# Slots of a counted graph layer put in order of segment size, and their byte parts cut out by one shift with three amounts

## The chip, the cores and the metric

One core of a Trainium2 chip runs the whole program. The metric is the device time of one execution in microseconds (us), median of three runs. For the kernel before these are 1352.64, 1352.75 and 1355.45 us. The profile is of a further execution, which took 1350.42 us; its recorded span is 1348.7 us, so 1.7 us lie outside the records.

## The reference

12,500 nodes have rows of 128 features. Each of 200,000 edges, sorted by destination, sends the normalized row of its source through one of four matrices to its destination:

```python
h = jnp.maximum(_layernorm(x, axis=-1), 0.0)
for i in range(4):
    mask = (edge_types == i)[:, None]
    msgs = msgs + jnp.where(mask, h[src] @ W[i] + b[i], 0.0)
x = x + jax.ops.segment_sum(msgs, dst, num_segments=N)
```

Destinations are drawn as `12500 * u**2`, so low node numbers have many edges and high ones few.

## The kernel before, in words

The edges are cut into 1563 chunks of 128. The last 995 chunks are *gathered*: GpSimd (POOL) fetches 128 rows of the normalized table `htab` per chunk by an indirect DMA (L614, 947 chunks; the first 48 take rows of x instead, L598), and TensorE (PE) sums them by one-hot matmuls (L667). Ten buffers of two chunks each hold the rows, so a gather waits until PE has used up the pair ten places earlier. The first 568 chunks are *counted*: for each of 1705 low nodes the kernel counts how often each source row and type occurs (one-hots on VectorE, L1092 and L1102; a matmul, L1127; a copy of the counts by ScalarE, L1135) and multiplies the counts by the table (from L1233 on).

What is counted together is a *slot*: one chunk seen from one unit of nodes. A unit is one node, or two or three neighbouring nodes whose counts share one 32-bit word, a byte each. Six segments of nodes follow each other in node order, with these sizes of a unit: nodes 0 to 3 size 1 (up to 16 chunks each), 3 to 117 size 3 (up to 12), 117 to 393 size 1, 393 to 462 size 3 (two chunks), 462 to 1036 size 2, 1036 to 1705 size 3. There are 850 units and 1035 slots. Slots are numbered in blocks (L145 to L152): first chunk k = 0 of all segments, then k = 1 of those that have it, and so on to k = 15. From k = 2 on a block of size 1 (nodes 0 to 3) and a block of size 3 (nodes 3 to 117) take turns, down to blocks of one slot.

`make_slots` fills the slots before the counting can begin. Three of its steps matter here:

- `runs(a, z)` (L957 to L966) cuts a stretch of slots into runs of one size, joining neighbours of equal size.
- `pick_out` (L968) works on three stretches of slots, 0 to 425 and 425 to 850 twice each and 850 to 1035 once. After its matmuls (L975, L978) it evicts each run apart: a square on ScalarE (ACT) into `off`, since the middle of the unit depends on the size (L986), then a compare-and-multiply on VectorE (DVE) into `packed` or `mask` (L987).
- `unpack` (L999) works on four pieces, slots 0 to 41, 41 to 317, 317 to 676 and 676 to 1035. It makes columns of constants for the counting (L1002 to L1022), then a matmul sums the edges of each type into a 12-row result (L1028). For each run, ScalarE casts the sums to integers (`ints`, L1036), VectorE takes the bytes out by a mask, a shift in place, a mask, a shift, a mask (L1041 and L1040, five instructions for size 3 and three for size 2), and ScalarE copies them to `cnt12` and adds them up on the way (L1043, two records each: the copy and the read of its accumulator). A run of size 1 goes straight from the sums to `cnt12`.

At the end a matmul with the bias per piece of a segment (L1059) and a copy (L1063) fill the first sums `acc`. All of this is written ahead of the main part. In the main part PE, VectorE and ScalarE work in the order of the program text; ahead of it a list scheduler that builds the program lays out each engine's queue, and may set instructions of the main part between those of the slots. The table (L532, L558, L568, L574) and three groups of raw rows (L725 and around it) are made in the same stretch of time. `gates` hold nineteen pairs of gathers back until marked instructions of `pick_out` and `unpack` are done.

Of the kernel before, what the change touches and what calls it, by code (L numbers as in the profile page):

```python
# [35 lines left out]
F32 = mybir.dt.float32  # L36
# [5 lines left out]
I32 = mybir.dt.int32  # L42
U16 = mybir.dt.uint16
AF = mybir.ActivationFunctionType
ALU = mybir.AluOpType
# [5 lines left out]
P = 128  # L51
# [37 lines left out]
def kernel(  # L89
# [10 lines left out]
    nc = tc.nc  # L100
    N, D = x.shape
    E = src.shape[0]
    NT, _, DO = w.shape
# [7 lines left out]
    N3 = 3 * NT  # L111
# [11 lines left out]
    ND = int(N * q**2 + 5 * 2 * q * N * (q * (1 - q) / E) ** 0.5) // 8 * 8 + 8  # L123

    def chunks_of(d, n):

        m = E * (((d + n) / N) ** 0.5 - (d / N) ** 0.5)
        return max(1, -(-int(m + ODDS * m**0.5) // P))

    ONES = next(d for d in range(0, ND, 3) if chunks_of(d, 1) == 1)  # L130
    TWOS = next(d for d in range(ONES, ND, 3) if chunks_of(d, 2) == 1)
    THREES = next(d for d in range(TWOS, ND, 2) if chunks_of(d, 3) == 1)
    NTWO = (THREES - TWOS) // 2
    HEAVY = next(d for d in range(0, ND, 3) if E * (((d + 1) / N) ** 0.5 - (d / N) ** 0.5) < 4 * P)
    parted = [(d, k) for d in range(HEAVY) for k in range(0, chunks_of(d, 1), 3)]
    LONE = next(n for n in range(min(NTWO - len(parted), TWOS - ONES), -1, -1) if (TWOS - ONES - n) % 3 == 0)
    AFTER = ONES + LONE
    ND += -(ND - THREES) % 3
    assert 0 < HEAVY < ONES <= AFTER <= TWOS < THREES < ND < 2047
    segs = []  # L140
    for d0, d1, size in ((0, HEAVY, 1), (HEAVY, ONES, 3), (ONES, AFTER, 1), (AFTER, TWOS, 3), (TWOS, THREES, 2), (THREES, ND, 3)):
        segs.append((sum(n for _, n, *_ in segs), (d1 - d0) // size, d0, size, [chunks_of(d, size) for d in range(d0, d1, size)]))
    UNITS = sum(n for _, n, *_ in segs)
    blocks = {}
    NS = 0  # L145
    for k in range(max(segs[0][4])):
        for s in range(len(segs)):
            n = sum(c > k for c in segs[s][4])
            if n:
                assert all(c > k for c in segs[s][4][:n])  # L150
                blocks[k, s] = NS, n
                NS += n  # L152
    assert (1, 2) not in blocks and segs[2][2:4] == (ONES, 1)
    LONE0 = blocks[0, 2][0]
    LONE1 = LONE0 + LONE

    def weight_at(c):
        return c if c < LONE0 else c - LONE

    ends_in = [12, 8, 4, 3]  # L160
    FULL = (TM - sum(ends_in)) // G
# [11 lines left out]
    size_of = lambda d: next(size for _, n, d0, size, _ in segs if d0 <= d < d0 + n * size)  # L173

    def slot_at(k, d):
        s = next(s for s in reversed(range(len(segs))) if d >= segs[s][2])
        return blocks[k, s][0] + (d - segs[s][2]) // segs[s][3]

    def slots_of(u):

        got = []
        u = list(zip(u, (1.0, 256.0, 65536.0)))
        if u[0][0] is not None and size_of(u[0][0][0]) > 1:
            d = u[0][0][0]
            size = size_of(d)
            got += [(slot_at(k, d), None) for k in range(chunks_of(d, size))]
            del u[:size]
        for v, by in u:
            if v is not None:
                d, k0 = v  # L190
                got += [(slot_at(k, d), by) for k in range(k0, min(k0 + 3, chunks_of(d, 1)))]
        return got
# [115 lines left out]
    prep = early.enter_context(tc.tile_pool(name="prep", bufs=1))  # L308
# [159 lines left out]
    nc.vector.tensor_copy(minus_h, minus)  # L468
    minus_1 = prep.tile([1, P], F16, name="minus_1")
    nc.vector.memset(minus_1, -1.0)  # L470
    mids = prep.tile([P, 3], F32, name="mids")
    for n in range(3):
        nc.vector.memset(mids[:, n : n + 1], -n / 2)
# [426 lines left out]
    def make_slots(dix):  # L900

        def pieces(a, z, of=512):
            n = -(-(z - a) // of)
            return [(a + (z - a) * i // n, a + (z - a) * (i + 1) // n) for i in range(n)]

        d1 = dix.tile([P, NS], F16, name="d1")
# [38 lines left out]
        for u0, n, _, _, caps in segs:  # L945
            i = 0
            while i < n:
                m = sum(c == caps[i] for c in caps)
# [8 lines left out]
        def runs(a, z):  # L957
            got = []
            for (_, s), (c0, n) in blocks.items():
                r0, r1, size = max(a, c0), min(z, c0 + n), segs[s][3]  # L960
                if r0 < r1:
                    if got and got[-1][2] == size:
                        r0 = got.pop()[0]
                    got.append((r0, r1, size))
            return got
# [33 lines left out]
        def unpack(a, z, shared):  # L999
            n = z - a  # L1000
            xi = dix.tile([P, 512], I32, name="xi")[:, :n]
            nc.vector.tensor_single_scalar(xi, packed[:, a:z], 256.0, op=ALU.mult)  # L1002
            hk = dix.tile([P, 512], I32, name="hk")[:, :n]
            nc.vector.tensor_single_scalar(hk, xi, 10, op=ALU.arith_shift_right)
            marks.append(nc.vector.tensor_copy(hkT[:, a:z], hk).ins)
            lo = dix.tile([P, 512], I32, name="lo")[:, :n]
            nc.vector.tensor_single_scalar(lo, xi, 255, op=ALU.bitwise_and)
            marks.append(nc.vector.tensor_single_scalar(loT[:, a:z], lo, -1.0, op=ALU.add).ins)
            if shared:
                by = byT[:, weight_at(a) : weight_at(a) + n]  # L1010
                nc.vector.tensor_single_scalar(xi, xi, 768, op=ALU.bitwise_and)
                nc.vector.tensor_single_scalar(xi, xi, float(1 << 18), op=ALU.mult)
                nc.vector.tensor_single_scalar(by.bitcast(I32), xi, float(127 << 23), op=ALU.add)
            nc.vector.tensor_single_scalar(hk, hk, NT - 1, op=ALU.bitwise_and)
            ohs = []
            for t in range(NT):
                is_t = dix.tile([P, 512], BF16, name="sel", bufs=2 * DENSE)[:, :n]
                of, like, op = (hk, t + 1.0, ALU.is_equal) if t < NT - 1 else (hkT[:, a:z], 0.5, ALU.is_gt)
                if shared:
                    one = nc.vector.scalar_tensor_tensor(is_t, of, like, by, op0=op, op1=ALU.mult)  # L1020
                else:
                    one = nc.vector.tensor_single_scalar(is_t, of, like, op=op)  # L1022
                ohs.append(is_t)
            marks.append(one.ins)
            yield True
            pn = x_ps.tile([N3, 512], F32, name="pt")
            for t in range(NT):
                nc.tensor.matmul(pn[:, :n], pick_a[:, t, :], ohs[t], start=(t == 0), stop=(t == NT - 1))  # L1028
            for r0, r1, size in runs(a, z):
                k, s, c0 = next((k, s, c0) for (k, s), (c0, m) in blocks.items() if c0 <= r0 < c0 + m)  # L1030
                w0 = at_nodes[k, s] + (r0 - c0) * size
                to = cnt12[:, w0 : w0 + (r1 - r0) * size]
                of = pn[:, r0 - a : r1 - a]
                if size > 1:
                    ints = dix.tile([N3, 512], I32, name="ints")[:, : r1 - r0]
                    nc.scalar.copy(ints, of)  # L1036
                    of = dix.tile([N3, 3 * 512], I32, name="parts", bufs=2)[:, : (r1 - r0) * size]
                    for m in range(size):
                        if m:
                            nc.vector.tensor_single_scalar(ints, ints, 8, op=ALU.arith_shift_right)  # L1040
                        nc.vector.tensor_single_scalar(of[:, m::size], ints, 255, op=ALU.bitwise_and)  # L1041
                i = len(some_of)
                some_of.append(nc.scalar.activation(to, of, AF.Copy, accum_out=some[:, i : i + 1]))  # L1043

        for r0, r1 in ((0, LONE0), (LONE0, LONE1), (LONE1, NS)):
            for a, z in pieces(r0, r1):
                yield from unpack(a, z, r0 != LONE0)
                yield True
# [4 lines left out]
        for s, (_, n, d0, size, _) in enumerate(segs):  # L1053
            for a, z in pieces(0, n * size):
                pn = x_ps.tile([P, 512], F32, name="pt")
                todo = [(at_nodes[k, r], m * size) for (k, r), (_, m) in blocks.items() if r == s and m * size > a]
                for i, (w0, m) in enumerate(todo):
                    m = min(m, z)
# [333 lines left out]
    slots = mid.enter_context(tc.tile_pool(name="slots", bufs=1, side="right"))  # L1392
    loT = slots.tile([P, NS], F32, name="loT")
    hkT = slots.tile([P, NS], F32, name="hkT")
    byT = slots.tile([P, NS - LONE], F32, name="byT")
    building = ExitStack()
    dix = building.enter_context(tc.tile_pool(name="dix", bufs=1, side="right"))
    to_slots = make_slots(dix)
    work = None
    dense_out = False  # L1400
# [299 lines left out]
    with tc.If(rv > 0):  # L1700
        with tc.tile_pool(name="slow", bufs=1) as slow, tc.tile_pool(name="slow_ps", bufs=1, space=PSUM) as slow_ps:
# [31 lines left out]
            with tc.For_i(0, T, 1) as t:  # L1733
                d1 = slow.tile([P, 1], F32, name="d1")
# [88 lines left out]
```

## Time and profile before

| what | value |
|---|---|
| median of 3 runs | 1352.75 us |
| profiled execution, whole | 1350.42 us |
| profiled execution, span | 1348.7 us |
| PE, share of the span busy | 90% |
| VectorE (DVE) | 80% |
| ScalarE (ACT) | 79% |
| POOL | 71% |
| DMA | 322.56 MB at a mean of 239 GB/s |

A share over the whole span says little here, because the program has stages. From the start to about 87 us the table is made; then slots and the first rows are made and counted; from about 165 us on counting, table products and gathers run beside each other until the end. Groups of instructions are listed by line with their count, busy time, mean duration and the idle time of the engine just ahead of them; a window view gives the busy time of each engine in a stretch; a timeline gives each instruction's start, its duration and, in brackets, how long its engine had been idle and who ended that. A start stands first in a row of the timeline, then the duration, both in us; runs of equal instructions are merged with a count.

### The profile page before, as it was taken

The numbers are of one execution on the slowest core, as the hardware profiler recorded it, in microseconds if no ns is written. First come the engines' busy times: TensorE is split into PE (matmuls) and PEld (weight loads), VectorE is DVE, ScalarE is ACT, GpSimd is POOL, SyncE is SP. The second block draws the span as 40 slices with busy tenths as digits, with TensorE's granted clock in tenths as the row PEclk, the third lists the DMA queues.
The fourth block names the chain that finished last, engine by engine and source line by source line (L and its number), as shares of the span: only waits on it lengthen the run. The fifth ranks groups of instructions, "written<-read, shape, count | busy, mean of one in ns | idle before, by whom it ended". The sixth has DMA issues, their size and how long they took to land. (4 is left out here: it accounts for less than half of the span.)

```text
span 1348.7 us, 30484 instructions
## 1 busy us (share of the span) xinstructions
PE 1219.8 (90%) x9211; PEld 879.8 (65%) x9211; DVE 1078.0 (80%) x5297; ACT 1068.3 (79%) x1893; POOL 956.0 (71%) x1035
## 2 busy tenths in 40 slices
PE   4875875799999999999999999999999999999975
PEld 1433654477777777777777777776676777667753
DVE  8996476977898898898988888788878888776532
ACT  6894743598998998989889888888978888778731
POOL 7735454677777777777777777777777777777774
PEclk9995677799999999999999999999999999999996
DMA  8743299598888888888788887878878887778952
GB/s 249 231 152 110 59 313 324 164 286 256 278 266 264 278 251 258 257 270 278 240 260 257 261 248 251 259 242 254 252 228 253 254 254 233 241 222 266 325 145 79
DMA packets 184630, 322.56 MB, mean 239 GB/s; under 512 B 30243, under 2 KB 82524, under 8 KB 184460
## 3 DMA queue, kind: packets, MB, share of 16 engines
q1 hardware_dynamic: 132716, 214.63, 48.9%
q0 software_dynamic: 46992, 96.30, 25.0%
q10 hardware_dynamic: 4752, 9.64, 1.8%
q8 instruction: 73, 1.20, 0.4%
q14 instruction: 97, 0.79, 0.2%
HBM read 294.78 MB, written 25.67 MB: 238 GB/s over the span
## 5 line engine op out<-in xcount | busy, mean ns | idle before, releaser
L614 POOL DMA_INDIRECT hm<-htab,srcT x947 | 902.3, 953 | 356.0 <-issue 189.8
L1195 ACT ACTIVATE dec<-counts 128x1116 fp32r<-128x1116 uint8 (+1 forms) x594 | 676.2, 1161 | 5.0 <-PE pa L1233 4.6
L1092 DVE TENSOR_SCALAR o<-iota_w,hkT 128x392 bf16<-128x392 f16 x1035 | 422.6, 408 | 115.7 <-PE pt L1127 112.7
L1233 PE MATMUL pa<-dec,hs 128*128 128x372 f32 x1764 | 389.1, 354 | 0.0
L1241 PE MATMUL pa<-counts,hs 128*128 128x372 fp8e4 x1764 | 341.6, 327 | 5.6 <-ACT sd L1279 5.6
L1135 ACT CAST counts<-pt 128x396 int32<-128x396 f32 x571 | 285.2, 519 | 42.1 <-PE pt L1127 22.5
L1233 PEld LDWEIGHTS pa<-dec,hs 128*128 128x128 f32 x1764 | 301.8, 188 | 13.8
L1127 PE MATMUL pt<-o,o 128*128 128x396 bf16 x1035 | 277.1, 340 | 16.9 <-DVE o L1102 11.4
L1241 PEld LDWEIGHTS <-hs 128*128 128x128 f16 x1764 | 164.5, 96 | 118.3 <-issue 9.1
L1102 DVE TENSOR_SCALAR o<-iota_b,loT,byT 128x128 bf16<-128x128 bf16 x730 | 239.3, 328 | 0.0
L756 DVE TENSOR_TENSOR ring<-ring,py 128x18 f32 (+6 forms) x912 | 158.6, 174 | 60.6 <-issue 16.1
L667 PEld LDWEIGHTS <-hm 128*128 128x128 f16 x2841 | 146.1, 100 | 87.3 <-DMA hm<-htab,srcT 23.6
L667 PE MATMUL ps<-oh,hm 128*128 128x72 bf16 (+7 forms) x2841 | 182.7, 200 | 17.8 <-DMA hm<-htab,srcT 17.3
L657 ACT ACTIVATE sb<-ps 128x288 f32<-128x288 f32 (+8 forms) x237 | 103.3, 436 | 111.4 <-PE py L693 90.3
L632 DVE TENSOR_SCALAR oh<-iota_b,keyT 128x72 bf16<-128x72 bf16 (+7 forms) x947 | 161.6, 259 | 8.6 <-PE ps L667 8.5
L693 PE MATMUL py<-sb,wsb 128*128 128x288 f32 (+6 forms) x456 | 123.9, 416 | 0.0
L1127 PEld LDWEIGHTS <-o 128*128 128x128 bf16 x1035 | 81.9, 99 | 55.0 <-DVE o L1102 17.8
L693 PEld LDWEIGHTS py<-sb,wsb 128*128 128x128 f32 x456 | 85.4, 198 | 22.5 <-issue 0.9
L1102 DVE TENSOR_SCALAR o<-iota_b,loT 128x128 bf16<-128x128 bf16 x305 | 83.3, 273 | 0.0
L598 POOL DMA_INDIRECT hx<-in_x_dram,srcT x48 | 46.4, 967 | 20.2 <-issue 10.8
L688 ACT CAST cnt<-pt 128x288 bf16<-128x288 f32 (+10 forms) x62 | 25.9, 418 | 42.0 <-PE pt L684 37.2
L1263 PE MATMUL pa<-counts,hs 128*128 128x156 fp8e4 x294 | 31.2, 261 | 18.7 <-DMA hs<-htab 18.5
(252 smaller groups left out, 819.3 us busy)
## 6 DMA issues: line engine op xcount, KB each, us to landing
hs<-dtab SPq DMA_DIRECT2D x576, 288.0 KB
hm<-htab,srcT POOLq DMA_INDIRECT x947
htab<-h SPq DMA_DIRECT2D x32, 288.0 KB
hs<-htab SPq DMA_DIRECT2D x32, 288.0 KB
dtab<-dec ACTq DMA_DIRECT2D x32, 288.0 KB
xo<-in_x_dram SPq DMA_DIRECT2D x23, 256.0 KB
out_dram<-xo SPq DMA_DIRECT2D x23, 256.0 KB
hm<-in_x_dram SPq DMA_DIRECT2D x18, 192.0 KB
```

The costliest lines, as they stand in the source:

```text
L614: one = nc.gpsimd.indirect_dma_start(out=hm[:, (i - h0) * D3 : (i - h0 + 1) * D3], out_offset=None, in_=htab, in_offset=bass.IndirectOffse ...
L632: nc.vector.tensor_scalar(oh[:, i, :], iota_b[:, :K], keyf[:, at : at + 1], None, ALU.is_equal)
L667: nc.tensor.matmul(ps[:, i - i0, :], rows(i, c), oh[:, i, :], start=(c == 0), stop=(c == 2))
L693: nc.tensor.matmul(py[:, :g, :], wsb[:, t, :], sb[0][:, :g, t, :], start=False, stop=(t == NT - 1))
L756: nc.vector.tensor_tensor(to, to, of(i), ALU.add)
L1092: one = nc.vector.tensor_scalar(o2[:, k, :NB].rearrange("p (r n) -> p r n", r=ROWS), iota_w, hkT[:, s : s + 1], None, ALU.is_equal)
L1102: one = nc.vector.tensor_scalar(o1[:, k], iota_b, loT[:, s : s + 1], by, ALU.is_equal, ALU.mult)
L1127: one = nc.tensor.matmul(pb, o1, o2, start=first, stop=last)
L1135: lambda i=i, pb=pb: nc.scalar.copy(counts[:, :, i * NT : (i + 1) * NT], pb.rearrange("p (b t) -> p b t", t=NT))
L1195: nc.scalar.activation(decoded[n][:, : j1 - j0, :nv].rearrange("p j (m v) -> p j m v", m=3), by_digit[:, j0:j1, : nu * NT * 4].rearrange(" ...
L1233: nc.tensor.matmul(to.rearrange("p (m v) -> p m v", m=3), row.bitcast(F32R)[:, D // 2 :], decoded[j // DS][:, j % DS, :nv].rearrange("p (m ...
L1241: nc.tensor.matmul(to.rearrange("p (m v) -> p m v", m=3), row[:, :D], counts[:, j, : nu * NT * 4].rearrange("p (v m) -> p m v", m=4)[:, :3 ...
```

## The change

The six segments stand in another order, with all of one size together: size 2 (nodes 462 to 1036) first, then the three of size 3 (3 to 117, 393 to 462, 1036 to 1705), then the two of size 1 (117 to 393, 0 to 3). The blocks of later chunks follow the same idea: behind the 850 units come the later chunks of nodes 0 to 3 (26 slots, size 1, so that they continue the stretch of size 1 ahead of them), then all later chunks of size 3 (159 slots). `unpack` takes four pieces again: slots 287 to 571 (size 3), 0 to 287 (size 2), 571 to 876 (size 1, without the weight `byT`, which is 29 columns shorter now) and 876 to 1035 (size 3). The rule of `runs` is the same; the stretches that it finds are others. Worked out from the text: `pick_out` meets 10 runs in its five jobs in place of 37, `unpack` 4 runs in place of 30 (three with bytes in place of 16).

The second edit is in `unpack`: a small table `shifts` (0, 8, 16 in each of 12 rows) is made once by POOL, and in place of three or five instructions one shift with two tensors writes all bytes, and one mask follows.

```diff
-    for d0, d1, size in ((0, HEAVY, 1), (HEAVY, ONES, 3), (ONES, AFTER, 1), (AFTER, TWOS, 3), (TWOS, THREES, 2), (THREES, ND, 3)):
+    for d0, d1, size in ((TWOS, THREES, 2), (HEAVY, ONES, 3), (AFTER, TWOS, 3), (THREES, ND, 3), (ONES, AFTER, 1), (0, HEAVY, 1)):
...
-    for k in range(max(segs[0][4])):
-        for s in range(len(segs)):
-            n = sum(c > k for c in segs[s][4])
...
+    for k, s in (
+        *((0, s) for s in range(len(segs))),
+        *((k, len(segs) - 1) for k in range(1, max(segs[-1][4]))),
+        *((k, s) for k in range(1, max(map(max, (of[4] for of in segs)))) for s in range(len(segs) - 1)),
+    ):
+        n = sum(c > k for c in segs[s][4])
...
-    LONE0 = blocks[0, 2][0]
-    LONE1 = LONE0 + LONE
+    PAIRS = segs[0][1]
+    LONE0 = segs[4][0]
+    LONE1 = UNITS + sum(segs[5][4]) - HEAVY
+    LONES = LONE1 - LONE0
...
+    shifts = prep.tile([N3, 3], I32, name="shifts")
+    nc.gpsimd.iota(shifts, pattern=[[8, 3]], base=0, channel_multiplier=0)
...
-                    for m in range(size):
-                        if m:
-                            nc.vector.tensor_single_scalar(ints, ints, 8, op=ALU.arith_shift_right)
-                        nc.vector.tensor_single_scalar(of[:, m::size], ints, 255, op=ALU.bitwise_and)
+                    nc.vector.tensor_tensor(
+                        of.rearrange("p (i m) -> p i m", m=size),
+                        ints.unsqueeze(2).to_broadcast([N3, r1 - r0, size]),
+                        shifts[:, :size].unsqueeze(1).to_broadcast([N3, r1 - r0, size]),
+                        ALU.arith_shift_right,
+                    )
+                    nc.vector.tensor_single_scalar(of, of, 255, op=ALU.bitwise_and)
...
-        for r0, r1 in ((0, LONE0), (LONE0, LONE1), (LONE1, NS)):
+        for r0, r1 in ((PAIRS, LONE0), (0, PAIRS), (LONE0, LONE1), (LONE1, NS)):
```

More of the change, by code (lines that the diff above doesn't have):

```diff
@@ L145 @@
     NS = 0
-    for k in range(max(segs[0][4])):
-        for s in range(len(segs)):
-            n = sum(c > k for c in segs[s][4])
[L149 to L153, printed above, removed]
-    LONE0 = blocks[0, 2][0]
-    LONE1 = LONE0 + LONE
+    for k, s in (
[4 more added lines that the diff above has]
+        n = sum(c > k for c in segs[s][4])
+        if n:
+            assert all(c > k for c in segs[s][4][:n])
+            blocks[k, s] = NS, n
+            NS += n
+    PAIRS = segs[0][1]
+    LONE0 = segs[4][0]
+    LONE1 = UNITS + sum(segs[5][4]) - HEAVY
+    LONES = LONE1 - LONE0
+    assert max(segs[4][4]) == max(segs[0][4]) == max(segs[3][4]) == 1
     def weight_at(c):
-        return c if c < LONE0 else c - LONE
+        return c if c < LONE0 else c - LONES
     ends_in = [12, 8, 4, 3]
@@ L175, in slot_at @@
     def slot_at(k, d):
-        s = next(s for s in reversed(range(len(segs))) if d >= segs[s][2])
+        s = next(s for s, (_, n, d0, size, _) in enumerate(segs) if d0 <= d < d0 + n * size)
         return blocks[k, s][0] + (d - segs[s][2]) // segs[s][3]
@@ L1394 @@
     hkT = slots.tile([P, NS], F32, name="hkT")
-    byT = slots.tile([P, NS - LONE], F32, name="byT")
+    byT = slots.tile([P, NS - LONES], F32, name="byT")
     building = ExitStack()
```

## The prediction

> **What bounds the kernel now.** I read the page first, then busy time by stage, then POOL's timeline, then the timelines of ACT and DVE in the stretch that stood out. The columns of the stage view are the stretch, its length, the busy time (and count) of PE, of PE's weight loads, of DVE, ACT and POOL, the granted PE clock, the DMA share and GB/s.
>
> ```profile
> span 1348.7 us, 30484 instructions
> ```
>
> ```profile
> 60.00:87.00 27.00, 20.90 (x81) 9.01 (x79) 26.07 (x119) 26.97 (x73) 7.85 (x9) 1.00 0.61 210
> 87.00:102.00 15.00, 11.33 (x77) 7.35 (x76) 14.68 (x80) 13.53 (x55) 8.22 (x9) 0.86 0.31 99
> 102.00:113.00 11.00, 9.83 (x42) 6.33 (x42) 8.48 (x37) 3.53 (x15) 9.17 (x7) 0.50 0.74 244
> 113.00:133.00 20.00, 6.58 (x39) 3.34 (x38) 13.49 (x73) 8.92 (x68) 7.13 (x8) 0.50 0.17 44
> 133.00:165.00 32.00, 25.55 (x156) 20.84 (x156) 10.76 (x48) 23.20 (x66) 13.86 (x15) 0.59 0.22 57
> 258.00:1326.00 1068.00, 1036.67 (x8063) 761.94 (x8061) 870.90 (x4282) 908.12 (x1413) 808.09 (x853) 0.99 0.81 252
> ```
>
> Each stage has its own limit. From 60 to 87 ACT is full (26.97 of 27 us, the table) and DVE nearly so. From 258 to 1326 us PE is busy 97% and POOL issues 853 gathers in 1068 us, 1.25 us each. From 113 to 133 us nothing is full: PE works 6.58 of 20 us, DMA stands at 17%, and DVE and ACT hand work to each other. POOL's timeline says what that stretch costs.
>
> ```profile
> 121.32 0.95 POOL L614 DMA_INDIRECT hm<-htab,srcT  x1 [0.30 <-issue]
> 133.02 0.94 POOL L614 DMA_INDIRECT hm<-htab,srcT  x1 [10.76 <-PE ps L667]
> ...
> 161.87 0.94 POOL L614 DMA_INDIRECT hm<-htab,srcT  x1 [2.64 <-PE ps L667]
> ...
> 258.05 0.94 POOL L614 DMA_INDIRECT hm<-htab,srcT  x1 [3.28 <-PE ps L667]
> ```
>
> The view of waits gives POOL's for 122 to 163 us in one row (total, times, longest):
>
> ```profile
> POOL hm L614 <- PE ps L667: 26.1, 6, 10.8
> ```
>
> A gather of 0.95 us and 0.30 us of issue make the 1.25 us: behind 258.05 POOL never waits longer than that issue, so the end is set by when this last unbroken run starts. Until then its long waits are for PE's use of earlier rows (L667), never for its own work. So a microsecond by which the main part starts earlier should be a microsecond off the end. The main part starts when the slots are done:
>
> ```profile
> 113.03 0.28 ACT L1036 CAST ints<-pt 12x174 int32<-12x174 f32 x1
> ...
> 115.73 0.64 ACT L1043 ACTIVATE cnt<-parts 12x522 bf16<-12x522 int32 x1 [2.27 <-DVE parts L1041]
> ...
> 128.99 0.13 ACT L1036 CAST ints<-pt 12x1 int32<-12x1 f32 x1
> ...
> 130.03 0.21 ACT L1043 ACTIVATE cnt<-parts 12x3 bf16<-12x3 int32 x1 [0.76 <-DVE parts L1041]
> 130.15 0.18 ACT L1043 ACTIVATION_READ_ACCUMULATOR cnt<-parts 12x1 f32 x1
> 130.24 0.13 ACT L1036 CAST ints<-pt 12x1 int32<-12x1 f32 x1
> ...
> 133.38 0.49 ACT L1135 CAST counts<-pt 128x396 int32<-128x396 f32 x1
> ```
>
> ```profile
> 129.16 0.14 DVE L1041 TENSOR_SCALAR parts<-ints 12x1 int32<-12x1 int32 x1 [0.41 <-ACT ints L1036]
> ...
> 129.86 0.14 DVE L1041 TENSOR_SCALAR parts<-ints 12x1 int32<-12x1 int32 x1
> ```
>
> One run of a single slot takes a round: cast at 128.99, five dependent instructions on DVE from 129.16 to 130.00, the copy at 130.03, the next cast at 130.24. That is 1.25 us for one column. The last piece has 24 such runs, and its chain lasts from 113.03 to the first cast of counts at 133.38, 20.35 us.
>
> **The change part by part.** The groups, from 40 to 135 us (count, busy us, mean ns, idle ahead):
>
> ```profile
> L1041 DVE TENSOR_SCALAR parts<-ints 12x1 int32<-12x1 int32 (+12 forms) x47 | 9.1, 195 | 6.3 <-ACT ints L1036 5.5
> L1040 DVE TENSOR_SCALAR ints<-ints 12x1 int32<-12x1 int32 (+12 forms) x31 | 5.4, 174 | 0.8
> L987 DVE SCALAR_TENSOR_TENSOR packed<-off,pt 128x1 f32<-128x1 f32 (+14 forms) x30 | 4.6, 181 | 1.7 <-ACT off L986 1.6
> L986 ACT ACTIVATE off<-pt,mids 128x3 f32<-128x3 f32 (+14 forms) x37 | 9.2, 291 | 2.1 <-DVE packed L987 1.8
> L1063 ACT COPY acc<-pt 128x287 f32<-128x287 f32 (+6 forms) x8 | 2.7, 337 | 2.5 <-PE pt L1059 2.5
> ```
>
> ```profile
> L708 DVE TENSOR_TENSOR ohf<-iota_f,keyT 128x768 fp32r<-128x768 f32 x1 | 0.9, 944 | 0.0
> L1007 DVE TENSOR_SCALAR lo<-xi 128x359 int32<-128x359 int32 x2 | 0.7, 326 | 0.0
> ```
>
> *New byte step.* 78 instructions (47 and 31, 14.5 us busy) become three shifts and three masks, on 852, 574 and 477 elements of 12 rows. No shift with two tensors is in the trace. Its nearest row is L708, which also reads two stretched operands: 944 ns for 768 elements, in proportion 1.05, 0.71 and 0.59 us. A mask is at most in proportion to L1007: 0.77, 0.52 and 0.43 us. Together 4.1 us. From below, all six could be as cheap as the mean of the old ones, 195 ns, 1.2 us; from above I double to 8.2 us, because integers and 12 rows are not the row's case. I take 4.1 us, nearest to rows of the same access and size. For a large run the edit by itself even loses a little (five instructions of 284 elements, 0.26 us each by L1007, are 1.3 us against 1.8); what gains is that there are three runs and not sixteen.
>
> *The chain at the end.* The last piece has one run now. By rows: cast 0.28, shift 0.59, mask 0.43, copy of 477 elements 0.64 (the row for 522), accumulator 0.18. The copies of `acc` still to come behind it, four of eight because a buffer of PSUM serves each in turn, take (2.7 + 2.5) / 8 = 0.65 us each with their wait, 2.6. With some 0.2 us for hand-overs that is 4.9 us in place of 20.35: **15.4 us** off. With the shift doubled it is 14.4.
>
> *Ahead of 113 us.* 27 of the 37 pairs of square and compare go. DVE loses the idle time of the stage 102 to 113, 11 minus 8.48 = 2.5 us, most of it the 1.6 us behind L986 in the row of L987: **2.5 us**. Of its busy time the 27 take 27 x 0.18 = 4.9 by their means, but the ten that stay are larger and cover the same slots, and small ones overlap; I take **1.2 us** (from 0 to 3). On ACT the first two jobs, which stand among the work on the table, lose six of ten squares: at 0.29 each 1.7; some filled idle moments, so **1.0 us** earlier for the table. The byte step costs as much as before there: 18 old instructions of about 0.19 against the first two new pairs, 3.05; nothing either way. Sum 4.7 us.
>
> *Moved.* The first counted batch takes units of the last segment, whose slots come with the first piece now, so its one-hots can be made sooner. That is worth nothing while DVE is full, and up to 4 us if they leave the last pieces' way. The gates of the gathers keep their number, three marks per piece and four pieces; the wait at 133.02 is for PE, so they are not last. In the main part no instruction changes in number: units and batches are the same, only slot numbers differ.
>
> *At nothing.* One iota on POOL at the start:
>
> ```profile
> 2.00 0.15 POOL L455 IOTA cidx_i<- 128x5 int32 x1
> ...
> 4.31 1.11 POOL L598 DMA_INDIRECT hx<-in_x_dram,srcT  x1 [1.26 <-ACT srcT L349]
> ```
>
> Such a one takes 0.15 us and hides in POOL's wait of 1.26; uncovered it costs 0.15.
>
> *What is late next.* The six waits of 26.1 us hold 6 x 0.3 of issue, so POOL stood 24.3 us for PE. Without any of it the gather of 161.87 could start at 137.6 by POOL's own rate; PE, 20.1 us earlier, releases its buffer for 141.8. So PE still comes last there, by 4.2 us, and POOL's later run starts earlier by the whole shift.
>
> *Sum.* 15.4 + 4.7 = 20.1 us. The profiled execution would go from 1348.7 + 1.7 = 1350.4 to 1330.3; its like among the runs has a median 2.3 us higher, so I put 1352.75 - 20.1 = **1332.6 us**.
>
> *The clock.* Two more rows, same columns:
>
> ```profile
> 104.00:108.00 4.00, 3.90 (x22) 3.06 (x22) 3.09 (x17) 1.38 (x6) 3.39 (x3) 0.50 0.76 243
> 164.00:168.00 4.00, 3.68 (x38) 3.19 (x38) 3.90 (x17) 2.71 (x7) 2.89 (x4) 1.00 0.28 75
> ```
>
> PE gets half its clock at 104 although it is busy 3.90 of 4 us, and the whole of it at 164; I let the slow stretch move along unchanged. [...]
>
> **The rivals.** *POOL takes over.* If the gathers were bound by their own rate from 122 on, only the first wait would be won, 10.76 - 0.3 = 10.5 us: 1342.3. For it: POOL sets the pace later. Against: five more waits for PE follow, to 161.87, with 15.3 of the 26.1 us.
>
> *The clock returns early.* From 133 to 165 PE is busy 25.55 us at 0.59, 15.1 us at full clock; ACT's 23.20 us of work then bound the stage of 32, so up to 8.8 us more: 1323.8.
>
> *Slower.* DVE works its queue in order. A large shift set early in it waits for ACT's cast, and ACT is full from 60 to 87 with the table; behind the shift stands the last split of each table block (L574), so the table would wait too. If DVE stood 25 us there, the result is 1352.75 - 20.1 + 25 = 1357.7; it decides from 20.1 us of standing. Against: work on the slots stood in DVE's queue there before, with squares of ACT to wait for, and DVE was busy 26.07 of 27 us.
>
> *It doesn't do what it says.* If the runs did not merge, or the next stage had its own start, the time stays 1352.75. The count of runs follows from the text, so this is small.
>
> **How the numbers follow.** Forecast 0.75, POOL 0.08, clock 0.10, slower 0.04, nothing 0.03. The forecast's own terms reach from 14.4 + 2.5 = 16.9 to 15.4 + 6.5 + 4 = 25.9 us, 1326.9 to 1335.9. The range takes in POOL's and the clock's case with a microsecond around them: 1322.5 to 1343.5. 0.2% is 2.7 us, about what a measurement can tell; faster 0.93, same 0.03, slower 0.04.
>
> **What would show it.** Squares of `pick_out`: 10; casts to `ints`: 3; shifts with two tensors: 3 of about 1.05, 0.71 and 0.59 us. The first cast of counts near 113 instead of 133.38, no round of 1.25 us left, POOL's unbroken run from about 238, and the span near 1328.6. Wrong would be: DVE standing still inside 60 to 87, POOL waiting as long as before ahead of its run, or an unchanged 258.05 with the slots done early.

## The result, and the profile after

The changed kernel takes 1334.27 us (median of 4 runs, 1332.94 to 1339.23) where the kernel before took 1353.35 us beside it (4 runs, 1352.64 to 1355.45): a ratio of 0.9863 with a 95% interval of 0.9834 to 0.9892, 19.1 us less, near the forecast of 1332.6. The profiled execution is the slowest of the four, 1339.23 us. In the changed kernel the lines of the program lie seven to ten further down: the squares are L993, the casts to integers L1043, the shift L1045, the mask L1051, the copies to `cnt12` L1053, the matmuls of a piece L1035, the use of gathered rows L674.

The page's first line, then the same stages as in the prediction:

```profile
span 1337.2 us, 30299 instructions
```

```profile
60.00:87.00 27.00, 24.20 (x106) 11.20 (x103) 26.26 (x115) 25.30 (x65) 9.90 (x10) 1.00 0.60 215
87.00:102.00 15.00, 12.05 (x67) 8.75 (x67) 14.87 (x62) 12.04 (x36) 6.95 (x5) 0.85 0.28 98
102.00:113.00 11.00, 7.31 (x29) 3.91 (x30) 5.82 (x26) 3.03 (x9) 8.87 (x8) 0.50 0.21 55
113.00:133.00 20.00, 15.71 (x107) 11.25 (x106) 11.38 (x50) 15.37 (x45) 14.92 (x17) 0.50 0.68 206
133.00:165.00 32.00, 27.55 (x218) 22.85 (x218) 16.67 (x68) 17.12 (x48) 18.48 (x19) 0.70 0.37 102
258.00:1326.00 1068.00, 1031.49 (x8022) 759.78 (x8022) 865.17 (x4245) 898.54 (x1401) 803.96 (x849) 0.99 0.81 251
```

From 113 to 133 us PE now works 15.71 us where it worked 6.58. But the stage ahead, 102 to 113, did not get fuller: DVE is busy 5.82 of 11 us, against 8.48 before. The timelines say why. First ACT, its casts and the end of the slots:

```profile
97.37 0.37 ACT L1043 CAST ints<-pt 12x284 int32<-12x284 f32 x1
...
108.05 0.39 ACT L1043 CAST ints<-pt 12x287 int32<-12x287 f32 x1 [4.27 <-PE pt L1035]
...
114.97 0.28 ACT L1043 CAST ints<-pt 12x159 int32<-12x159 f32 x1 [0.39 <-PE pt L1035]
...
118.69 0.51 ACT L1145 CAST counts<-pt 128x396 int32<-128x396 f32 x1
```

From the last piece's cast to the first cast of counts it is 118.69 - 114.97 = 3.72 us, where it was 20.35. Yet the last piece's cast itself comes 1.9 us later than before (113.03). DVE's timeline shows what stands ahead of it:

```profile
97.96 1.02 DVE L1045 TENSOR_TENSOR parts<-ints,shifts 12x852 int32<-12x852 int32 x1
...
99.13 0.58 DVE L1051 TENSOR_SCALAR parts<-parts 12x852 int32<-12x852 int32 x1
...
102.99 0.30 DVE L1012 CAST hkT<-hk 128x305 f32<-128x305 int32 x1
108.47 0.74 DVE L1045 TENSOR_TENSOR parts<-ints,shifts 12x574 int32<-12x574 int32 x1 [5.18 <-ACT ints L1043]
...
115.28 0.65 DVE L1045 TENSOR_TENSOR parts<-ints,shifts 12x477 int32<-12x477 int32 x1 [0.56 <-ACT ints L1043]
```

DVE stands for 5.18 us at the second shift. It waits for ACT's cast of 108.05, and that cast waited 4.27 us for PE. PE's queue at that moment:

```profile
103.83 0.29 PE L743 MATMUL pa<-cntr,b 12*128 12x160 bf16 x1 [0.65 <-ACT cntr L740]
104.05 0.41 PE L1035 MATMUL pt<-sel,pick_a 128*12 128x287 bf16 x1
104.39 0.90 PE L745 MATMUL pa<-sbr,wsb 128*128 128x160 f32 x2
105.22 0.41 PE L1035 MATMUL pt<-sel,pick_a 128*12 128x287 bf16 x1
105.55 0.90 PE L745 MATMUL pa<-sbr,wsb 128*128 128x160 f32 x2
106.38 0.41 PE L1035 MATMUL pt<-sel,pick_a 128*12 128x287 bf16 x1
106.72 0.90 PE L745 MATMUL pa<-sbr,wsb 128*128 128x160 f32 x2
107.55 0.41 PE L1035 MATMUL pt<-sel,pick_a 128*12 128x287 bf16 x1
```

The four matmuls of the piece take turns with the last product of raw group 0 (L745), 0.90 us a pair, behind a matmul that waited for ACT. Meanwhile everything that the last two pieces need of DVE stands in its queue behind the shift.

POOL's timeline ends the reading, with its last wait of over three microseconds, and the row of the view of waits for 122 to 163 us:

```profile
144.87 0.95 POOL L621 DMA_INDIRECT hm<-htab,srcT  x1 [4.04 <-PE ps L674]
...
244.77 0.94 POOL L621 DMA_INDIRECT hm<-htab,srcT  x1 [3.44 <-PE pt L1137]
```

```profile
POOL hm L621 <- PE ps L674: 9.8, 5, 4.0
```

The 10.76 us wait is gone, waits for PE stay (between the two rows shown also 7.14 us ahead of 186.88 and 8.91 ahead of 221.03). The unbroken run starts at 244.77, 13.3 us earlier than 258.05, and the span ends 1092.4 us behind it (1090.65 before).

### The profile page after: what moved, and what is told of

Read it like the earlier page. It is cut to its first block, busy times and chain, and to the rows that moved or that the text cites. A ratio compares the mean times of both kernels' runs of the same rounds, so it can differ in the third digit from the quotient of the medians.

```text
span 1337.2 us, 30299 instructions
## 1 busy us (share of the span) xinstructions
PE 1222.0 (91%) x9211; PEld 882.6 (66%) x9211; DVE 1069.5 (80%) x5198; ACT 1057.7 (79%) x1801; POOL 958.8 (72%) x1036
## 4 chain that ended last, share of the span: by engine, by line
PE 71%; DMA 11%; DVE 8%; ACT 5%; issue 3%; POOL 1%; DVEq 0%; SPq 0%; POOLq 0%; ACTq 0%
PE pa L1243 19%; PE pa L1251 18%; PE pt L1137 10%; PE py L700 8%; DMA hm<-htab,srcT 6%; PE ps L674 6%; DMA hs<-htab 2%; DVE o L1102 2%; PE pt L1296 2%; DVE o L1112 2%; DVE ring L763 1%; ACT dec L1205 1%; PE ps L732 1%; POOL hm L621 1%; ACT h L539 1%
## 5 line engine op out<-in xcount | busy, mean ns | idle before, releaser
L674 PEld LDWEIGHTS <-hm 128*128 128x128 f16 x2841 | 146.3, 100 | 87.8 <-DMA hm<-htab,srcT 24.0
L674 PE MATMUL ps<-oh,hm 128*128 128x72 bf16 (+7 forms) x2841 | 182.2, 200 | 18.3 <-DMA hm<-htab,srcT 16.5
L605 POOL DMA_INDIRECT hx<-in_x_dram,srcT x48 | 47.6, 992 | 21.4 <-issue 10.2
```

The lines of the kernel that those rows point to most:

```text
L674: nc.tensor.matmul(ps[:, i - i0, :], rows(i, c), oh[:, i, :], start=(c == 0), stop=(c == 2))
```

## The experiments

A table first, from the timelines of the profiled executions, since the same few times are asked of each kernel (us): where the table ends (the start of its last split on DVE), ACT's first and last cast to integers, the first cast of counts, POOL's last wait of over 3 us, the span.

| kernel | table | first cast | last cast | counts | POOL | span |
|---|---|---|---|---|---|---|
| before | 87.96 | 94.46 | 113.03 | 133.38 | 258.05 | 1348.7 |
| after | 90.47 | 97.37 | 114.97 | 118.69 | 244.77 | 1337.2 |
| after, again | 89.64 | 96.53 | 114.13 | 117.86 | 246.00 | 1337.0 |
| order alone | 88.12 | 95.03 | 110.30 | 114.45 | 240.04 | 1331.5 |
| order alone, again | 92.03 | 98.93 | 114.21 | 118.35 | 241.87 | 1334.1 |
| byte step alone | 90.17 | 96.67 | 114.42 | 125.45 | 248.52 | 1339.9 |
| product later | 90.05 | 96.94 | 111.17 | 116.26 | 246.30 | 1337.3 |
| ten cuts | 89.00 | 95.90 | 113.50 | 121.00 | 248.54 | 1339.8 |
| bytes in place | 89.80 | 96.70 | 111.48 | 114.26 | 240.54 | 1333.3 |
| both | 90.59 | 97.50 | 108.80 | 111.71 | 236.53 | 1326.9 |

**The changed kernel again**, with no edit, to see the spread.

> The changed kernel once more, for a second profile and a narrower interval. Theory (the chain of tiny runs was removed, the rest of the forecast's front part was lost to the granted PE clock standing at half around 48 us, by chance): ratio 0.985 to 0.988, and if the clock in 44 to 52 us is 1.00 this time, the last split of the table ends near 88 us instead of 90.9 and the first cast of counts comes near 116 instead of 118.7 us. Rival (the change itself makes the table late): last split at 90.9 us again, whatever the clock.

1337.74 us (4 runs, 1336.41 to 1338.98), a ratio of 0.9879 (0.9861 to 0.9896) to the kernel before, 1353.21 us (11 runs). So two samples of one kernel have medians 3.5 us apart, and the gain is 15.5 to 19.1 us. The stretch from the first cast to the last is 17.60 us in both traces to the hundredth. The theory is borne out only in part: the clock was full from 44 to 60 us this time, but the last split ended at 90.06 us (89.64 and 0.42), nearer the rival's 90.9 than the theory's 88, and the first cast of counts came at 117.86, not 116. This execution had two spells at half clock earlier, at about 27 to 30 and 37 to 41 us (0.92 as a mean from 0 to 44 us).

**The order alone**: the new order of segments with the old byte step.

```diff
-                    nc.vector.tensor_tensor(
-                        of.rearrange("p (i m) -> p i m", m=size),
...
-                    nc.vector.tensor_single_scalar(of, of, 255, op=ALU.bitwise_and)
+                    for m in range(size):
+                        if m:
+                            nc.vector.tensor_single_scalar(ints, ints, 8, op=ALU.arith_shift_right)
+                        nc.vector.tensor_single_scalar(of[:, m::size], ints, 255, op=ALU.bitwise_and)
```

> New order of segments and pieces, old byte step (three or five instructions a run). Theory (merging the runs is the gain, the byte step is neutral for large runs): 13 byte instructions of about 0.25 us in place of 6 that take 3.8 us together, time within 1 us of the changed kernel, near 1334. Rival (the byte step brings the gain): at least half of the gain is lost, 1344 or more.

1333.32 us (5 runs, 1331.96 to 1334.2), ratio 0.9849 (0.9834 to 0.9864); no run as slow as any of the changed kernel beside it. Once more, in another set of runs:

> The new order with the old byte step once more, since one execution of it had no half clock between 44 and 52 us where all others had. Theory (the queue that results is what makes it faster than the changed kernel: 15.27 us from the first cast of sums to the last against 17.60 in three runs of the new byte step): again 15.3 us for that stretch, a first cast of counts at 114 to 116 us by where the table ends, and 0.984 to 0.987 of the kernel before. Rival (it was the clock): the stretch is 15.3 us but the table ends 1.5 to 2.5 us later, and the time is that of the changed kernel, 0.988.

1335.62 us (5 runs, 1330.7 to 1337.9), ratio 0.9859 (0.9835 to 0.9883). The order alone has all of the gain; the byte step adds nothing to it and may cost up to 4 us. The stretch between the casts is 15.27 and 15.28 us against 17.60: the builder's scheduler lays PE's queue out another way there, three of the piece's four matmuls ahead of the raw group's product, not among it. PE's timeline in the order-only kernel:

```profile
100.53 0.40 PE L1033 MATMUL pt<-sel,pick_a 128*12 128x287 bf16 x1
...
101.02 0.40 PE L1033 MATMUL pt<-sel,pick_a 128*12 128x287 bf16 x1
...
101.67 0.40 PE L1033 MATMUL pt<-sel,pick_a 128*12 128x287 bf16 x1
102.00 0.31 PE L741 MATMUL pa<-cntr,b 12*128 12x160 bf16 x1
102.24 0.90 PE L743 MATMUL pa<-sbr,wsb 128*128 128x160 f32 x2
103.07 0.40 PE L1033 MATMUL pt<-sel,pick_a 128*12 128x287 bf16 x1
```

DVE stands at the first byte instruction of this piece too, for 3.64 us in place of 5.18, so the wait comes with the merged runs and not with the shift alone:

```profile
103.93 0.36 DVE L1046 TENSOR_SCALAR parts<-ints 12x287 int32<-12x287 int32 x1 [3.64 <-ACT ints L1041]
```

The table ends at 88.12 in the one execution and at 92.03 in the other, of one and the same kernel. The granted clock between 44 and 60 us differs, first the earlier one, then the later:

```profile
44.00:48.00 4.00, 2.84 (x9) 0.98 (x8) 4.00 (x39) 3.97 (x11) 3.85 (x23) 1.00 0.67 236
48.00:52.00 4.00, 3.43 (x17) 1.63 (x15) 4.00 (x25) 3.78 (x10) 2.87 (x4) 1.00 0.71 220
```

```profile
44.00:48.00 4.00, 3.98 (x11) 1.29 (x11) 3.62 (x21) 2.55 (x6) 3.55 (x17) 0.63 0.47 167
48.00:52.00 4.00, 3.46 (x9) 1.30 (x8) 3.65 (x37) 3.20 (x8) 3.08 (x4) 0.50 0.64 200
```

**The byte step alone**, in the old order of segments (the second edit of the change and not the first).

> Old order, new byte step: 16 runs with bytes of two instructions in place of five. Theory: a round of one slot drops from 1.25 us by three dependent instructions of 0.175, to 0.72, so that the chain of 20.35 us loses about 6 to 7 us: near 1346. Rival (the byte step brings the gain): near 1334.

1344.91 us (6 runs, 1341.74 to 1346.87), ratio 0.9937 (0.9922 to 0.9951): 8.3 us less than before. The chain behind the last cast is 125.45 - 114.42 = 11.03 us in place of 20.35, with the same 24 runs of slots, 12 of them with bytes. ACT's copies in its last rounds:

```profile
121.55 0.21 ACT L1048 ACTIVATE cnt<-parts 12x9 bf16<-12x9 int32 x1 [0.19 <-DVE parts L1046]
...
122.31 0.21 ACT L1048 ACTIVATE cnt<-parts 12x6 bf16<-12x6 int32 x1
...
123.07 0.19 ACT L1048 ACTIVATE cnt<-parts 12x3 bf16<-12x3 int32 x1
```

A pair of rounds (one with bytes, one without) takes 0.76 us and no longer 1.3: two instructions on DVE for a round, not five. So the byte step is worth something where there are many runs, and nothing where the order has left one. The gain of the order alone (1353.21 - 1333.32 = 19.9 and 1353.67 - 1335.62 = 18.1 us) and that of the byte step alone, 8.3 us, do not add up to that of the change, since they shorten the same rounds.

**Ten cuts**: the changed kernel with the last piece's single run cut into one of 149 slots and ten of one slot.

```diff
-            for r0, r1, size in runs(a, z):
+            cuts = runs(a, z)
+            if z == NS:
+                ((r0, r1, size),) = cuts
+                cuts = [(r0, r1 - 10, size)] + [(r, r + 1, size) for r in range(r1 - 10, r1)]
+            for r0, r1, size in cuts:
```

In one set of four kernels, this one among them, the kernel before itself took 1641.90 us (11 runs, 1637.04 to 1646.21), with every engine standing still at places for which the trace names no cause, so that the runs of this set are compared with that time alone.

> The changed kernel with the 159 slots of the last piece cut into one run of 149 and ten runs of one slot; the work computed is the same. Theory (each round of cast, shift, mask and copy stands in the chain to the first cast of counts, and the chain passes one to one to the end): in the kernel of the byte edit alone the last small rounds took 0.76 us each (copies at 121.55, 122.31 and 123.07), so ten add 5 to 7.6 us to the chain of 3.7 us, the first cast of counts comes at 123 to 126 and the time is 5 to 8 us above the changed kernel, near 1343. Rival (the chain has slack behind it, as POOL or the scheduler fills the stretch with other work): less than 2 us, near 1337.

1627.33 us (4 runs), ratio 0.991 (0.9886 to 0.9934). Then:

> The same kernel as in the run of ten cuts, asked again, since on that chip the kernel before took 1641.9 us and all engines stood for several us at a time where the trace names no cause (PE 5.15 us ahead of 140.61). Where the kernel before takes about 1353 us, the first theory (rounds stand in the chain, and the chain passes one to one) gives a first cast of counts at 123 to 126 us and 5 to 8 us more than the changed kernel, so 0.992 to 0.994 of the kernel before. The rival (slack behind the chain) gives 0.987 to 0.988, as the changed kernel.

1339.37 us (5 runs, 1338.96 to 1341.81) beside 1354.71 for the kernel before, ratio 0.989 (0.9869 to 0.9911). ACT's timeline has the last piece's cast, three of the ten rounds, and the end:

```profile
113.50 0.27 ACT L1047 CAST ints<-pt 12x149 int32<-12x149 f32 x1 [0.39 <-PE pt L1035]
...
117.77 0.21 ACT L1057 ACTIVATE cnt<-parts 12x3 bf16<-12x3 int32 x1 [0.15 <-DVE parts L1055]
...
118.31 0.21 ACT L1057 ACTIVATE cnt<-parts 12x3 bf16<-12x3 int32 x1 [0.20 <-DVE parts L1055]
...
118.71 0.21 ACT L1057 ACTIVATE cnt<-parts 12x3 bf16<-12x3 int32 x1
...
121.00 0.49 ACT L1149 CAST counts<-pt 128x396 int32<-128x396 f32 x1
```

The chain is 7.50 us, 3.8 longer than 3.72 for ten rounds: 0.38 us a round, less than the 0.5 to 0.76 expected, because the rounds overlap (two casts stand at 115.95 and 116.31 us, their copies at 116.72 and 117.11). The first cast of counts comes 2.3 to 3.1 us later than in the two traces of the changed kernel, POOL's run 2.5 to 3.8, the span ends 2.6 to 2.8 later. So the rounds are in the chain and the chain goes through to the end; but the times, 0.989 against 0.9863 and 0.9879, lie too close for their intervals to show it by themselves, and 0.989 is below the 0.992 to 0.994 that the theory asked for.

**The product later**: the last product of raw group 0 is issued in the main part, not ahead of it.

```diff
-    for _ in groups[0]:
-        pass
+    for _ in range(9):
+        next(groups[0])
...
-    raw_steps = n1[:2]
+    raw_steps = [lambda: next(groups[0], None)] + n1[:2]
```

> The changed kernel with the last product of raw group 0 (nine matmuls and their weight loads) taken out of the stretch in which slots are unpacked and put first among the raw steps of the main part. Theory (in the changed kernel PE's queue sets four of these matmul pairs between the four matmuls of the second piece of slots, and VectorE stands 5.2 us for it): first cast of counts 3 to 5 us earlier than in the changed kernel, of which 2.5 to 3.6 us are given back to PE's work in the next stage: 0 to 3 us faster than the changed kernel. Rival (VectorE's wait has another cause): first cast of counts unmoved and the time the same or up to 2 us longer.

1336.27 us (4 runs, 1331.51 to 1338.98), ratio 0.9859 (0.9839 to 0.988). DVE's wait fell from 5.18 to 1.68 us and the stretch between the casts from 17.60 to 14.23, but the time is that of the changed kernel; the profiled execution, the slowest of the four, loses the gain between 116 and 246 us. By itself this stays inconclusive.

**Bytes in place**: no shift and no mask; ACT's copy reads the bytes of the integers where they lie, and these have two buffers. What is computed is the same.

```diff
-                    of = dix.tile([N3, 3 * 512], I32, name="parts", bufs=2)[:, : (r1 - r0) * size]
-                    nc.vector.tensor_tensor(
...
-                    nc.vector.tensor_single_scalar(of, of, 255, op=ALU.bitwise_and)
+                    of = ints.bitcast(U8).rearrange("p (i b) -> p i b", b=4)[:, :, :size]
+                    to = to.rearrange("p (i m) -> p i m", m=size)
```

> The changed kernel without shift and mask: ScalarE's copy reads the bytes of the integers where they lie, as 8-bit numbers four bytes apart, so that VectorE has no part in it. Theory (VectorE stood 5.2 us in the changed kernel since its shift waits, in order, for ScalarE's cast and through it for PE, and then ran the shift and mask of the last piece, 1.0 us, in the chain): no wait of VectorE for that cast, the chain from the last cast of sums to the first cast of counts near 2.7 us, the first cast of counts 4 to 6 us earlier than 118, and the time near 1332. Rival 1 (it is PE that is late, and VectorE only waits beside it): 1 us earlier by the shorter chain, near 1336. Rival 2 (the clock's spells set it): anywhere, with no wait of VectorE and yet no gain.

1623.65 us (6 runs, 1617.78 to 1629.92), ratio 0.9879 (0.9855 to 0.9904), in the set where all was longer. Then:

> The same kernel as in the run of the bytes read in place, asked again for the same reason. Where the kernel before takes about 1353 us, the theory (VectorE's standing of 5.2 us and its shift and mask in the last chain are on the path) gives no wait of VectorE for the cast, a last chain near 2.7 us, a first cast of counts at 112 to 114 us and a time near 1331, 0.984 of the kernel before. Rival 1 (PE is late by itself): the first cast at 116 to 117 us and 0.987. Rival 2 (the clock's spells set it): a first cast earlier or later with the half clock between 44 and 60 us, whatever VectorE does.

1333.98 us (5 runs, 1329.55 to 1335.09), ratio 0.9841 (0.9817 to 0.9865). ACT's timeline:

```profile
96.70 0.37 ACT L1041 CAST ints<-pt 12x284 int32<-12x284 f32 x1
...
111.48 0.28 ACT L1041 CAST ints<-pt 12x159 int32<-12x159 f32 x1
111.80 0.60 ACT L1045 ACTIVATE cnt<-ints 12x477 bf16<-12x477 uint8 x1
...
114.26 0.49 ACT L1137 CAST counts<-pt 128x396 int32<-128x396 f32 x1 [0.33 <-PE pt L1129]
```

The copy of 477 bytes takes 0.60 us, as the copy of 477 integers did, and the chain is 2.78 us, as the theory had it. No instruction on the way to the last cast waits for ACT on DVE, the stretch is 14.78 us, the first cast of counts 3.6 to 4.4 us earlier, and the span 3.7 to 3.9 us shorter than in the two traces of the changed kernel. This execution had the half clock as well (0.66 and 0.50 between 44 and 52 us), and its table ended between those of the two traces of the changed kernel, so an earlier table is not what made the difference. From about 110 to 113.5 us, though, its clock was full where theirs was at half (from 102 to 113 us 0.63 as a mean, in both of theirs 0.50). From the last piece's first matmul to its cast it took 1.17 us (110.31 to 111.48), in the changed kernel 1.77 (113.20 to 114.97), so up to 0.6 us of the shorter stretch can be the clock's. The second buffer of the integers was not tried apart.

**Both**: bytes in place and the product later. With the old byte step the later product was tried too, in the longer set only:

> The new order with the old byte step, and the last product of raw group 0 moved from the stretch ahead of the main part into it. Theory (the wait of 3.64 us of VectorE in the order-only kernel comes from matmuls of a piece that stand between that product's in PE's queue): that wait falls to about 1.7 us as it did with the new byte step, the first cast of counts comes 1.5 to 2.5 us earlier, at 112 to 113, and the time is 1331 to 1332. Rival (the product is only moved and costs as much later, as the changed kernel with the same move showed): 1333, no difference from the order alone.

1621.03 us (6 runs), ratio 0.9888 (0.9863 to 0.9912), no more than the others there. The stretch between its casts is 14.03 us (118.25 to 132.28), 1.2 less than with the order alone; the ten cuts took 17.60 us in this set as well, so the stretch can be compared. With the bytes in place:

> The bytes read in place by ScalarE, and the last product of raw group 0 moved into the main part. Theory (that product's eight matmuls stand between those of the last pieces in PE's queue, 0.90 us each pair): the stretch from the first cast of sums to the last falls from 14.8 to about 12.5 us, the first cast of counts to 112 and the time to 1330 to 1332, 0.982 to 0.983 of the kernel before. Rival (the product is only moved, as in the run of the later tail): the first cast is earlier and the time is that of the bytes read in place alone, 0.984.

1327.07 us (5 runs, 1325.62 to 1331.78), ratio 0.9811 (0.9788 to 0.9833) to the kernel before: the fastest of all, and by the ratios 7 to 9 us below the changed kernel. Its ACT, its POOL and two windows:

```profile
97.50 0.38 ACT L1041 CAST ints<-pt 12x284 int32<-12x284 f32 x1
...
108.80 0.28 ACT L1041 CAST ints<-pt 12x159 int32<-12x159 f32 x1 [0.34 <-PE pt L1033]
...
111.71 0.49 ACT L1137 CAST counts<-pt 128x396 int32<-128x396 f32 x1 [0.33 <-PE pt L1129]
```

```profile
236.53 0.95 POOL L619 DMA_INDIRECT hm<-htab,srcT  x1 [3.15 <-PE pt L1129]
```

```profile
104.00:106.00 2.00, 2.00 (x14) 1.19 (x13) 2.00 (x11) 0.87 (x3) 1.52 (x2) 0.50 0.28 78
106.00:108.00 2.00, 2.00 (x12) 0.71 (x8) 2.00 (x9) 1.48 (x6) 1.56 (x2) 0.50 0.19 53
```

The four kernels make a square. From the first cast to the last it takes 17.60 us with shift and product, 14.23 without the product, 14.78 without the shift, 11.30 without either: 3.4 and 2.8 us apart, 6.3 together. So the shift with its mask in DVE's queue and the product in PE's are two costs, each worth about 3 us in the layouts that the scheduler gave these kernels (with the old byte step the product was worth 1.2). For the shift the better pair is the one without the product, 14.23 and 11.30, 2.9 us, where both have the half clock throughout (0.50 from 102 to 113 us). DVE and PE are both full from 104 to 108 us (2.00 of 2 us in each window) when both are gone.

**The pieces in order**: slots 0 to 287 unpacked ahead of 287 to 571.

```diff
-        for r0, r1 in ((PAIRS, LONE0), (0, PAIRS), (LONE0, LONE1), (LONE1, NS)):
+        for r0, r1 in ((0, PAIRS), (PAIRS, LONE0), (LONE0, LONE1), (LONE1, NS)):
```

> The changed kernel with the first two pieces of the unpacking in the order of their slot numbers, 0 to 287 first and 287 to 571 second. Theory A (the early piece is worth something, since the first counted units are of the last segment): up to 4 us slower than the changed kernel, 1337 to 1341. Theory B (what is late is the last piece, whichever of the others comes first): within 1 us of the changed kernel, and the first cast of counts at 116 to 119 us as there.

1624.92 us (6 runs, 1619.02 to 1628.73), ratio 0.9891 (0.9868 to 0.9915), in the longer set, where the changed kernel was not run. It stands where the others of that set stand; whether the early piece is worth a microsecond stays open.

## Why the prediction was right, and where it was not

*The chain at the end* is right: 15.4 us were forecast and 20.35 - 3.72 = 16.6 came off. Its sum of 4.9 us was 1.2 too much, because four of the six copies of `acc` start on ACT between 115.36 and 116.85 us, ahead of the copy to `cnt12` at 116.91, and not behind it. The reason is shown twice: the old order with fewer instructions a round loses 9.3 us of the chain, and ten rounds put back cost 3.8.

*Ahead of 113 us* is the step that failed. It gave 4.7 us; the last cast came 1.9 us later instead. Two terms of it are wrong. The table was to end 1.0 us earlier; it ended 2.5 us later. That goes with the clock and not with the order. Added up over windows of 0.25 us, the clock ahead of 60 us is at half for 0 us in one trace (the table ends at 88.12), 3.4 us in one (87.96, the kernel before), 6.8 us in five (89.00 to 90.59), 10.2 us in two (90.05 and 90.17) and 13.7 us in one (92.03). The pair at 10.2 us compares the orders: 90.17 is the byte step alone, with the old order and all its squares, 90.05 the product later, with the new order. So ACT's six squares bought nothing that shows.

The other two terms, 3.7 us of DVE's idle and busy time, showed as 18.57 - 17.60 = 1.0 us from the first cast to the last. Since the first pieces differ, the stretch from the table's end to the last cast is the fairer one: 25.07 us before and 24.50 after, 0.6 us. With the byte step alone it is 24.25, so fewer squares and compares gained nothing there. The waits for squares did go, but the shift's wait of 5.18 us took their place. That is the mechanism of the rival called slower, at another place and price: not between 60 and 87 us (DVE is busy 26.26 of 27 there) but at 103, where fewer and larger steps leave DVE nothing else ahead of the shift, and PE has the raw product in the way. The square of four kernels prices shift and product; why the scheduler's layout differs between the two byte steps was not tried.

*The new byte step* is right in its sizes. The shifts took 1.02, 0.74 and 0.65 us (forecast 1.05, 0.71, 0.59), the masks 0.58, 0.44 and 0.39 us, 3.8 us for the six in place of 4.1. That the edit by itself brings nothing for large runs is right as well. What the forecast left out is that the wait ahead of it is the cost, not the instruction.

*What is late next* holds in part. From POOL's unbroken run to the end it is 1090.4 to 1092.8 us in all ten traces of the table, so that part passes one to one. Between the first cast of counts and that run it does not: 14.7 us earlier became 13.3, and 11.5 at the end of the profiled execution. PE is what POOL waits for there (9.8 us in five waits), as forecast, and POOL did not take over.

*The clock* was to be slow for the same stretch, moved along. The stretch kept its length but did not move: the clock is at half for 54.6 us on end in both kernels, to 152.5 us before and to 152.0 after, while counting began 14.7 us earlier. Behind it the kernel before fell to half once more, so that from 157 to 165 us its clock is 0.64 and that of the changed kernel 1.00. The mean from 120 to 240 us is 0.71 before and 0.68 after, where PE is busy for 83.78 us, and an estimate from these three numbers is 3.7 us; that this is the missing 3.2 us is argued and not shown. The rival with the clock back early did not come: from 133 to 165 us the clock is 0.70, with PE busy 27.55 of 32 us, where the rival took it as full. No run shows what brings the clock back; that it would come back there was the author's assumption. In the kernel with both edits PE is busy for the whole of 104 to 108 us at 0.50. The clock differs between two executions of one program, too: of those of the order-only kernel one has no half clock ahead of 60 us, the other 13.7 us of it.

*At nothing*: the iota took 0.12 us beside POOL's wait, which stayed 1.26. *Moved*: open.

So the gain came from the chain, as forecast, but that the time fell within 2 us of the forecast is luck. The step ahead of 113 us missed by 6.6 us, and 3.2 us more were lost behind the first cast of counts, so the span of the profiled execution, the slowest of the four, fell by 11.5 us and not by 20.1. The signs say the same: 10 squares, 3 casts and 3 shifts as named, but the first cast of counts at 118.69 and not near 113, POOL's run at 244.77 and not 238, the span 1337.2 and not 1328.6. Without the 4.7 us the sum is 15.4, and the repeat gained 15.5; the 19.1 us of the first sample lie within what executions of one kernel differ by (1332.94 to 1339.23 us).

## What to carry to other kernels

Where a group of small results goes round between two engines, price the round and count the rounds: first make them fewer by ordering equal things together, and only then make each cheaper, for both save the same time once. Before an engine that works in order is given one large step in place of many small ones, look at what that step waits for and at what stands behind it (DVE stood 5.18 us here). And if another engine can read the bytes as they lie (ACT here, 0.60 us for 477 of them), the step can be left out.

## What the runs showed of the hardware

- ACT reads three bytes of each 32-bit word where they lie, in one copy, at the price of integers: 0.60 us for 477 elements of 8 bits, 0.59 for 477 integers in the changed kernel.
- With PE busy for 4.00 of 4 us (104 to 108 us, in the changed kernel and in the one with both edits) the clock stood at 0.50 all that time. In windows of 0.25 us, every spell at half clock that begins ahead of 258 us in the kernel before and in the changed kernel lasts 3.41 us or a whole multiple of it: 6.83, 13.66, 17.07 and 54.61 us. The order-only kernel is at 1.00 between 48 and 52 us in one execution and at 0.50 in the other, and its table ends 3.9 us apart.
- The kernel before took 1642 us in one set of runs and 1355 in the next. From 258 to 1326 us an instruction of POOL took 948 ns on the mean in the bytes-in-place kernel of that set (653.84 us for 690) and 947 ns in the changed kernel (803.96 us for 849, all gathers); the time lay in standing, such as 5.15 us of PE ahead of 140.61 with no releaser in that kernel's trace. Its cause is not known.
